# A graph layer on one Trainium2 core: 37 of 49 node blocks packed instead of 35, and sums of gathered tiles on an even beat

## The chip, the cores and the metric

The kernel runs on one core of one Trainium2 chip. The metric is the device time of one execution in microseconds; 7 executions of the kernel before have a median of 624.59 us (622.95 to 628.96). Lower is better.

## The reference, cut to what matters

6250 nodes with 128 features, 100,000 edges sorted by their target node, two kinds of edge.

```python
Xs = X[src]
m_data = Xs @ W_data.T + b_data
m_ctrl = Xs @ W_control.T + b_control
msg = jnp.where((edge_types == 0)[:, None], m_data, m_ctrl)
agg = jax.ops.segment_sum(msg, dst, num_segments=X.shape[0])
out = jax.nn.relu(agg + (X @ W_self.T + b_self))
x = _layernorm(x + out, axis=-1)
```

## The kernel before, in words

**Messages first.** Nodes are padded to 49 blocks of 128 rows. For each block the kernel multiplies x by both message weights in float32 (tile y, functions multiply, take, leave, last_part) and keeps each result as three bfloat16 parts that add up to it: the tile m3 in SBUF, and the same rows in a table in device memory, written by store. A row of 384 numbers is one node's message for one kind of edge. This build phase lasts for roughly the first 78 us.

**Then sums per target block.** Edges are sorted, so all edges of a target block lie in one window of 18 x 128 edges, of which some belong to its neighbours. There are two ways to sum a window.

- *Packed* blocks (the first 35, in 7 groups of 5). For a group, the fields of its edges are computed (edge_fields), one-hot tiles by source block are made on DVE (bucket_hots, tile hot_st), and ranks gives each edge a slot within its source block: PE adds into the accumulator acc with the constants tri and rest, DVE takes a maximum (slot, L584), 18 times in turn. fill_a and fill_b bring the edges into their slots (tile small, L621), fill_c copies them out (vs), writes them to device memory (packed), and lists the edges that found no slot, whose rows POOL fetches in one spill gather per group (mixed, L715). For each packed block the list is then read back to all partitions (rows, L739), compared to the partition number (L746), and used as weights: g_ps (gather, L775) picks the rows out of m3 with a matmul, ACT evicts them to gs (evict, L790), and add_up sums them into agg with the one-hot of the target (hot_d, L760). A block has 25 such rounds: 98 matmuls for g_ps and 100 for agg. Evictions may be given to DVE only in blocks of the last group (b >= STARTS[-1]).
- *Gathered* blocks (the last 14). For each of their 18 x 128 edges POOL fetches the message rows by an indirect DMA from the table (gather_rows, tile msg, L877, a ring of MB = 5 tiles), DVE makes a one-hot of the targets for six at a time (hot_g, L889), and gathered_sums adds the tile into agg_g with four matmuls.

All matmuls with 32 output rows go through by_columns (L231) in fours, one for each 32 columns of the weights. Every block adds its own term x @ W_self into its accumulator, and finish_blocks or finish_gathered sums its three parts (whole, L153), applies relu, adds x and takes the statistics; normalise scales and stores a group of blocks at a time.

**What sets the order.** Each part above is a Python generator that yields steps: a name, the engines that may run it with a cost, and the steps it needs. The class Order is a planner: it keeps a clock per engine (T is PE, V is DVE, A is ACT, G is POOL, S is SP), and among the steps that could start first takes the one with the earliest due time from due(). The order in which the steps are taken is the order of the instructions in each engine's queue. Nothing of the planner runs on the chip: its clocks only decide who stands ahead of whom. The constants that the change touches are BLOCK (due distance of packed blocks), PACE (due distance of gathered tiles, and before also the cost of a gather on POOL), and GROUPS, from which NPB (packed blocks), NG (gathered blocks) and the starts of the groups follow.

Of the kernel before, what the change touches and what calls it, by code (L numbers as in the profile page):

```python
# [27 lines left out]
KT = 18  # L28
# [4 lines left out]
ES = ER // RJ  # L33
EPS = 1e-05

GROUPS = (5,)*7
Q = max(GROUPS)
NPG = len(GROUPS)
NPB = sum(GROUPS)
NG = NB - NPB  # L40
STARTS = [sum(GROUPS[:i]) for i in range(NPG)]
R = 32
# [10 lines left out]
CH = 6  # L53
# [5 lines left out]
class Order:  # L59
# [10 lines left out]
    CLOSE = 0.1  # L70

    def __init__(self):
        self.free = dict.fromkeys("TVAGS", 0.0)
        self.end = {}

    def run(self, streams, due):
# [24 lines left out]
def step(name, costs, *needs, lag=0.0):  # L101
    return as_tuple(name), costs, [as_tuple(n) for n in needs], lag


def as_tuple(name):
    return name if isinstance(name, tuple) else (name,)
# [107 lines left out]
def sums_over_windows(ctx, tc, x, xt, edges, w, bias, table, packed, total,  # L214
                      add_parts, finish, load_rows, norm):
    nc = tc.nc
    V, A, G, T = nc.vector, nc.scalar, nc.gpsimd, nc.tensor
# [66 lines left out]
    for j in range(RJ):  # L284
# [17 lines left out]
    counted = {n: const.tile([P, P, n], BF16, name=f"count{n}")  # L302
               for n in sorted({DC, CH, *GROUPS})}
    tri = const.tile([P, P], BF16, name="tri")
# [77 lines left out]


    LEAD, BUILT = 6.0, 76
    BLOCK = 13.1
    PACE = 1.68
    AHEAD, FIRST = 26.0, 20

    def due(kind, *i):
# [35 lines left out]
        if kind in ("rows", "sel", "d", "g", "e", "s"):  # L425
            of = {"rows": 1, "sel": 1, "d": 2}.get(kind, NS)
            lead = {"rows": -9, "sel": -3, "d": -1, "g": 0, "e": 1, "s": 2}[kind]
            return BUILT + BLOCK * (i[0] + (i[1] / of if len(i) > 1 else 0)) + lead
        if kind in ("gh", "gm", "msg"):
            k = i[1] * CH if kind == "gh" else i[1]  # L430
            return BUILT + PACE * (i[0] * KT + k) + {"msg": 0, "gh": 2, "gm": 5}[kind]
        n = GROUPS[i[0]]
        end = BUILT + BLOCK * STARTS[i[0]] - (AHEAD if i[0] else FIRST)
        span = BLOCK * n if i[0] else 34.0
# [7 lines left out]
        if kind in ("two", "v"):  # L442
            c, k = (i[1], 0) if kind == "two" else divmod(i[1], KC)
# [71 lines left out]
    stored = [("table", g, t) for g in range(len(PARTS)) for t in range(2)]  # L515
# [337 lines left out]
    gathered = [(j, k) for j in range(NG) for k in range(KT)]  # L853
    idx = const.tile([P, NG, KT], I32, name="idx")
    rel_g = const.tile([P, NG, KT], BF16, name="rel_g")
    msgs, g_hots, kept = {}, {}, []
    GQ = -(-NG // -(-NG // Q))
    MB, XB = 5, 2

    def gathered_fields():  # L860
        yield step("idx", {"V": 1.8}, ("y", NB * 3 // 4), *[("win", b) for b in range(NPB, NB)])
# [10 lines left out]
    def gather_rows():  # L872
        for i, (j, k) in enumerate(gathered):
            free = [("gm", *gathered[i - MB])] if i >= MB else [*stored, "idx"]
            yield step(("msg", j, k), {"G": PACE}, *free, lag=3.0 - PACE)
            msgs[j, k] = late.tile([P, D3], BF16, name="msg", bufs=MB)
            G.indirect_dma_start(  # L877
                out=msgs[j, k], out_offset=None, in_=table[:, :],
                in_offset=bass.IndirectOffsetOnAxis(ap=idx[:, j, k : k + 1], axis=0),
            )  # L880

    def gathered_hots():
        chunks = [(j, c) for j in range(NG) for c in range(KT // CH)]
        for i, (j, c) in enumerate(chunks):

            free = [("gm", chunks[i - XB][0], chunks[i - XB][1] * CH + CH - 1)] if i >= XB else []
            yield step(("gh", j, c), {"V": 0.55}, ("msg", j, c * CH), ("counts", CH), *free)
            g_hots[j, c] = hot = late.tile([P, P, CH], BF16, name="hot_g", bufs=XB)
            V.tensor_tensor(hot, counted[CH],  # L889
                            rel_g[:, j, None, c * CH : c * CH + CH].to_broadcast([P, P, CH]),  # L890
                            op=ALU.is_equal)

    def gathered_sums():
        for j, k in gathered:
            free = [("agg", NPB + j)] if k == 0 else [("o", NPB + j)] if k == KT - 1 else []
            yield step(("gm", j, k), {"T": 0.165}, ("msg", j, k), ("gh", j, k // CH), *free)
            if k == 0:
                aggs[NPB + j] = ps_a.tile([P, D3], F32, name="agg_g")
            by_columns(aggs[NPB + j], g_hots[j, k // CH][:, :, k % CH], msgs.pop((j, k)),
                       start=k == 0, stop=k == KT - 1, skip_group_check=True)  # L900

    def finish_gathered():
        for j in range(NG):
            b = NPB + j
            yield step(("whole", b), {"V": 0.5}, ("gm", j, KT - 1))
            whole = add_parts(aggs.pop(b), work)
            yield step(("sum", b), {"V": 0.7}, ("whole", b))
            if j % GQ == 0:
                kept.append((late.tile([P, GQ, D], F32, name="h_g"),
                             work.tile([P, Q, 2], F32, name="mv_g")))  # L910
            h, mv = kept[-1]
            finish(h[:, j % GQ, :], whole, xss.pop(b))
            stats(mv[:, j % GQ, :], h[:, j % GQ, :], work)
# [14 lines left out]
    def close_build():  # L928
# [9 lines left out]
        normalise([(lambda g=g: (hs_[g], mvs[g]), STARTS[g] + q0, q0, n) for g, q0, n in PIECES], "p"), add_up(), gather(), evict(), to_hots(), bucket_hots(),  # L938
        multiply(), take(0, "yh", "y"), leave(0, "y1", "yh"),
        take(1, "ym", "y1"), last_part(), constants(), store(), close_build(), add_counts(),  # L940
        finish_gathered(), gathered_sums(), gathered_hots(), gather_rows(), gathered_fields(),
        normalise([(lambda i=i: kept[i], NPB + i * GQ, 0, min(GQ, NG - i * GQ))
                   for i in range(-(-NG // GQ))], "g"),
        load_own("p", list(range(NPB)), XS),
# [128 lines left out]
```

## Time and profile before

| What | Value |
|---|---|
| median of 7 executions | 624.59 us |
| the profiled execution's own time | 626.73 us |
| its span | 625.0 us |
| mean granted clock of TensorE over the span | 0.982 |

The profile is of one execution. A row of a group reads: line, engine, operation, output and inputs, shapes and count, then the busy time in us and the mean ns of one, then the idle time of that engine just before them with what ended it. PE is the matmul part of TensorE and PEld its weight loads; DVE, ACT, POOL and SP are the vector, scalar, GpSimd and sync engines. Ends of matmuls are modelled, so their starts say more than their lengths. A row of waits reads: who waited for whom, us in total, how often, the longest.

These groups of the page name the work of the gathered blocks and of the evictions:

```profile
L790 ACT CAST gs<-g_ps 128x384 bf16<-128x384 f32 x807 | 337.6, 495 | 148.3 <-PE g_ps L775 90.3
L877 POOL DMA_INDIRECT msg<-table,idx x252 | 283.7, 1126 | 201.8 <-PE g_ps L775 87.7
L231 PE MATMUL agg<-gs,hot_d 128*32 128x384 bf16 x3360 | 307.8, 337 | 18.7 <-ACT gs L790 11.3
```

### The profile page before, as it was taken

The numbers are of one execution on the slowest core, as the hardware profiler recorded it, in microseconds if no ns is written. First come the engines' busy times: TensorE is split into PE (matmuls) and PEld (weight loads), VectorE is DVE, ScalarE is ACT, GpSimd is POOL, SyncE is SP. The second block draws the span as 40 slices with busy tenths as digits, with TensorE's granted clock in tenths as the row PEclk, the third lists the DMA queues.
The fourth block names the chain that finished last, engine by engine and source line by source line (L and its number), as shares of the span: only waits on it lengthen the run. The fifth ranks groups of instructions, "written<-read, shape, count | busy, mean of one in ns | idle before, by whom it ended". The sixth has DMA issues, their size and how long they took to land.

```text
span 625.0 us, 26355 instructions
## 1 busy us (share of the span) xinstructions
PE 549.3 (88%) x11204; PEld 442.4 (71%) x11204; DVE 433.8 (69%) x967; ACT 420.2 (67%) x1003; POOL 292.5 (47%) x267
## 2 busy tenths in 40 slices
PE   6899878997989898898999899899898999878994
PEld 4455565776768776677868787778786887766883
DVE  4778794768575777767678766878677656447784
ACT  6644553667587766668767786677777777667784
POOL 1000016555556565655555664656645465465510
PEclk9899987999999999999999999999999999999998
DMA  3576764324334333344243443434334343335401
GB/s 104 151 221 182 228 234 134 108 70 155 95 110 130 113 105 116 118 134 147 66 162 114 143 123 108 120 113 142 119 118 130 114 142 118 118 108 161 141 13 43
DMA packets 60932, 79.19 MB, mean 127 GB/s; under 512 B 15760, under 2 KB 51371, under 8 KB 60807
## 3 DMA queue, kind: packets, MB, share of 16 engines
q1 hardware_dynamic: 47253, 49.14, 24.7%
q0 software_dynamic: 12400, 25.08, 14.2%
q10 hardware_dynamic: 1154, 3.21, 1.7%
q8 instruction: 89, 1.46, 0.9%
q14 instruction: 36, 0.29, 0.1%
HBM read 64.35 MB, written 13.05 MB: 124 GB/s over the span
## 4 chain that ended last, share of the span: by engine, by line
PE 77%; ACT 7%; DVE 6%; issue 5%; DMA 3%; SPq 1%; another core or an unknown queue 0%; ACTq 0%; DVEq 0%
PE agg L231 26%; PE g_ps L775 25%; PE acc L231 9%; PE agg_g L231 8%; PE small L621 6%; ACT gs L790 5%; PE y L465 2%; DVE hot_st L567 1%; DVE slot L584 1%; ACT h_p L189 1%; DMA rows<-packed 1%; DVE two L605 1%; DMA packed<-vs 1%; DMA msg<-table,idx 1%; ACT h_g L189 0%
## 5 line engine op out<-in xcount | busy, mean ns | idle before, releaser
L790 ACT CAST gs<-g_ps 128x384 bf16<-128x384 f32 x807 | 337.6, 495 | 148.3 <-PE g_ps L775 90.3
L877 POOL DMA_INDIRECT msg<-table,idx x252 | 283.7, 1126 | 201.8 <-PE g_ps L775 87.7
L775 PE MATMUL g_ps<-m,rows 128*32 128x384 bf16 x3430 | 335.5, 335 | 23.1 <-issue 11.3
L231 PE MATMUL agg<-gs,hot_d 128*32 128x384 bf16 x3360 | 307.8, 337 | 18.7 <-ACT gs L790 11.3
L231 PEld LDWEIGHTS <-hot_d 128*32 128x32 bf16 x3500 | 204.2, 137 | 59.3 <-issue 49.8
L775 PEld LDWEIGHTS <-rows 128*32 128x32 bf16 x3430 | 189.1, 138 | 53.0 <-issue 47.9
L584 DVE TENSOR_REDUCE slot<-acc 128x5 bf16<-128x490 f32 x126 | 83.7, 664 | 65.8 <-PE acc L231 31.7
L231 PE MATMUL agg_g<-msg,hot_g 128*32 128x384 bf16 x1008 | 106.6, 330 | 3.8 <-DMA msg<-table,idx 3.4
L760 DVE TENSOR_TENSOR hot_d<-count,to 128x1664 bf16<-128x1664 bf16 x70 | 74.5, 1066 | 12.7 <-PE agg L231 7.3
L621 PE MATMUL small<-hot_st,two 128*32 128x98 bf16 x1260 | 69.8, 290 | 2.2 <-issue 2.0
L231 PE MATMUL acc<-hot_st,tri 128*32 128x490 bf16 x504 | 61.4, 377 | 3.1 <-DVE hot_st L567 2.2
L621 PEld LDWEIGHTS <-two 128*32 128x32 bf16 x1260 | 56.4, 117 | 6.7 <-issue 4.9
L231 PE MATMUL acc<-hot_st,rest 128*32 128x490 bf16 x476 | 56.5, 380 | 4.4 <-DVE slot L584 3.5
L231 PEld LDWEIGHTS <-hot_g 128*32 128x32 bf16 x1008 | 52.8, 125 | 6.9 <-issue 5.7
L715 POOL DMA_INDIRECT mixed<-table,row_i x7 | 6.5, 934 | 95.7 <-PE g_ps L775 82.7
L153 DVE TENSOR_REDUCE whole<-agg 128x128 f32<-128x384 f32 x35 | 19.4, 555 | 44.8 <-PE g_ps L775 34.4
L476 ACT CAST m<-y 128x512 bf16<-128x512 f32 (+1 forms) x50 | 28.1, 577 | 31.0 <-PE y L483 23.1
L567 DVE TENSOR_TENSOR hot_st<-count,st_b 128x2940 bf16<-128x2940 bf16 x21 | 41.9, 2000 | 9.1 <-PE small L621 4.9
L746 DVE TENSOR_SCALAR rows<-rows,pid 128x3136 bf16<-128x3136 bf16 x35 | 36.1, 1033 | 2.5 <-DMA rows<-packed 2.4
L465 PE MATMUL y<-w_sb,xt 128*128 128x256 f32 x98 | 33.3, 426 | 0.0
L231 PEld LDWEIGHTS <-rest 128*32 128x32 bf16 x476 | 21.6, 100 | 12.6 <-issue 11.7
L790 DVE CAST gs<-g_ps 128x384 bf16<-128x384 f32 x33 | 17.9, 556 | 12.6 <-PE g_ps L775 10.4
(144 smaller groups left out, 437.8 us busy)
## 6 DMA issues: line engine op xcount, KB each, us to landing
rows<-packed SPq DMA_DIRECT2D x35, 784.0 KB
table<-m SPq DMA_DIRECT2D x10, 768.0 KB
msg<-table,idx POOLq DMA_INDIRECT x252
xt<-in_xt ACTq DMA_DIRECT2D x5, 512.0 KB
xt_p<-in_xt SPq DMA_DIRECT2D x35, 64.0 KB
xs_p<-in_x SPq DMA_DIRECT2D x35, 64.0 KB
out<-h_p SPq DMA_DIRECT2D x6, 320.0 KB
table<-m SPq DMA_DIRECT2D x2, 480.0 KB
```

Of the source, the lines that this page charges most:

```text
L153: nc.vector.tensor_reduce(whole, agg.rearrange("p (i c) -> p c i", i=3), axis=AX.X, op=ALU.add)
L231: T.matmul(out[c : c + 32], lhsT[:, c : c + 32], rhs, **flags)
L465: T.matmul(y[:, j, :], xts[g][:, b + j - at_part[g], :], w_sb[:, : 2 * D], start=j == 0, stop=False, skip_group_check=True)
L476: A.copy(part_of(b, n, i), ys[b][:, :n, :].rearrange("p b (t c) -> p t b c", t=2))
L567: V.tensor_tensor(hot, counted[n][:, None, 1 : NT + 1, :].to_broadcast([P, KC, NT, n]), fields[grp][2][:, c * KC : c * KC + KC, None, :].t ...
L584: V.tensor_reduce(slots[grp][:, k, :], by_q, axis=AX.X, op=ALU.max)
L621: T.matmul(vt[c0 : c0 + R, q // 2, :], two[:, k % KC, i, :, q], hot[:, k % KC, :, q], start=k == 0 and q < 2, stop=k == KT - 1, skip_group ...
L746: V.tensor_scalar(rows[b], rows[b], pid1, None, op0=ALU.is_equal)
L760: V.tensor_tensor(hot, counted[DC][:, :, :n], places[grp][:, q, None, c * DC : c * DC + n].to_broadcast([P, P, n]), op=ALU.is_equal)
L775: T.matmul(g_ps[t * R : (t + 1) * R, :D3], rows[b][:, :, s], m3[:, s, :], start=True, stop=True)
L790: (A.copy if e == "A" else V.tensor_copy)(gs[at], g_tiles.pop((b, g))[at, :D3])
L877: G.indirect_dma_start(out=msgs[j, k], out_offset=None, in_=table[:, :], in_offset=bass.IndirectOffsetOnAxis(ap=idx[:, j, k : k + 1], axis=0),
```

## The change

Two blocks more are packed (37) and two fewer gathered (12). The groups are now eight: two of four blocks, five of five, one of four. The planner gets a further clock, C, that belongs to no engine: a stream of beats takes PACE of it for each gathered tile, one after the other, and the sum of a gathered tile needs its beat. A gather costs POOL 1.25 in the planner's eyes, where it was PACE. The ring of gathered tiles has four places and not five, so a gather waits for the sum four back. BLOCK, PACE and the due time of gathered sums get other numbers.

```diff
-GROUPS = (5,)*7
+GROUPS = (4,)*2+(5,)*5+(4,)
...
-        self.free = dict.fromkeys("TVAGS", 0.0)
+        self.free = dict.fromkeys("TVAGSC", 0.0)
...
-    BLOCK = 13.1
-    PACE = 1.68
+    BLOCK = 12.7
+    PACE = 2.1
...
+        if kind in ("beat", "beating"):
+            return 0.0
...
-            return BUILT + PACE * (i[0] * KT + k) + {"msg": 0, "gh": 2, "gm": 5}[kind]
+            return BUILT + PACE * (i[0] * KT + k) + {"msg": 0, "gh": 2, "gm": 0}[kind]
...
-    MB, XB = 5, 2
+    MB, XB = 4, 2
...
-            yield step(("msg", j, k), {"G": PACE}, *free, lag=3.0 - PACE)
+            yield step(("msg", j, k), {"G": 1.25}, *free, lag=3.0)
...
+    def beats():
+
+        yield step("beating", {"C": 4.0}, *stored, "idx")
+        for i, (j, k) in enumerate(gathered):
+            yield step(("beat", j, k), {"C": PACE}, "beating")
...
-            yield step(("gm", j, k), {"T": 0.165}, ("msg", j, k), ("gh", j, k // CH), *free)
+            yield step(("gm", j, k), {"T": 0.165}, ("msg", j, k), ("beat", j, k), ("gh", j, k // CH), *free)
```

Lines of the changed kernel after the new rule in due() stand two lower than before (L775 is L777, L877 is L879).

What this does to the queues, at three places. First POOL, whose whole work after the start is gathers: msg rows for the gathered blocks, and one spill gather (mixed) per group. The lines with a minus are those of before.

```order
-L715 DMA mixed_146<-table,row_i_1182 32x384
-L877 DMA msg<-table,idx 128x384 x29
-L715 DMA mixed_147<-table,row_i_3056 32x384
-L877 DMA msg<-table,idx 128x384 x41
-L715 DMA mixed_146<-table,row_i_5325 32x384
+L717 DMA mixed_147<-table,row_i_1160 32x384
+L879 DMA msg<-table,idx 128x384 x19
+L717 DMA mixed_148<-table,row_i_2633 32x384
+L879 DMA msg<-table,idx 128x384 x25
+L717 DMA mixed_147<-table,row_i_4421 32x384
```

Between the spill gathers of the first groups there were 29 and 41 gathers, and now there are 19 and 25. In all, 252 gathers become 216, and 7 spill gathers become 8.

Second PE in the first packed block (agg), where the first gathered tile (msg) is summed into agg_g. Before:

```order
L775 MATMUL g_ps_1584<-m3_157,rows_1124 32x384
...
L231 LDWEIGHTS hot_g_1566
L231 MATMUL agg_g_1591<-msg_1434,hot_g_1566 32x384
...
L231 MATMUL agg_1339<-gs_1559,hot_d_1323 32x384
```

And now:

```order
L777 MATMUL g_ps_1670<-m3_159,rows_1081 32x384
...
L231 LDWEIGHTS hot_g_1645
L231 MATMUL agg_g_1677<-msg_1440,hot_g_1645 32x384
...
L231 MATMUL agg_1296<-gs_1620,hot_d_1307 32x384
```

The neighbours are of the same kind, but the place in the queue is later: 23 fours of g_ps, 19 of agg and 56 of acc stood ahead of this sum, and now 27, 23 and 62.

Third PE in the middle of the program. Each line stands for the first matmul of a four. Before, about a third of the way into the queue:

```order
L775 MATMUL g_ps_6083<-m3_157,rows_5198 32x384
...
L231 MATMUL agg_g_5730<-msg_5919,hot_g_6056 32x384
...
L231 MATMUL agg_g_5730<-msg_5971,hot_g_6056 32x384
...
L231 MATMUL agg_5943<-gs_6054,hot_d_5269 32x384
```

And now, at about the same place:

```order
L231 MATMUL agg_g_5478<-msg_6145,hot_g_6245 32x384
...
L777 MATMUL g_ps_6435<-m3_159,rows_5364 32x384
...
L777 MATMUL g_ps_6446<-m3_159,rows_5364 32x384
...
L777 MATMUL g_ps_6455<-m3_159,rows_5364 32x384
...
L231 MATMUL acc_6158<-hot_st_4978,tri_144 32x490
...
L231 MATMUL agg_g_5478<-msg_6209,hot_g_6245 32x384
```

Two gathered sums stood back to back there, which they did at 13 places in the program and now do at 4; between those shown now stand three rounds of the packed block, the copies of the group's slots and a rank step. A packed block in the middle had 7 to 9 gathered sums in its stretch of PE's queue, and now has 4 to 8, mostly 6. The last gathered sum stood 45 rounds of agg before the end of the queue, and now stands 25 before it.

More of the change, by code (lines that the diff above doesn't have):

```diff
@@ L940, in sums_over_windows @@
         take(1, "ym", "y1"), last_part(), constants(), store(), close_build(), add_counts(),
-        finish_gathered(), gathered_sums(), gathered_hots(), gather_rows(), gathered_fields(),
+        finish_gathered(), gathered_sums(), gathered_hots(), gather_rows(), gathered_fields(), beats(),
         normalise([(lambda i=i: kept[i], NPB + i * GQ, 0, min(GQ, NG - i * GQ))
```

## The prediction, made before the changed kernel had run

> **What bounds the kernel now.** I read the page first: which engine is busy, and through which engine the chain runs that ended last.
>
> ```profile
> span 625.0 us, 26355 instructions
> PE 549.3 (88%) x11204; PEld 442.4 (71%) x11204; DVE 433.8 (69%) x967; ACT 420.2 (67%) x1003; POOL 292.5 (47%) x267
> PE 77%; ACT 7%; DVE 6%; issue 5%; DMA 3%; SPq 1%; another core or an unknown queue 0%; ACTq 0%; DVEq 0%
> ```
>
> PE is the busiest engine and carries 77% of the chain. POOL, whose gathers are what the change spaces out, is busy for less than half. Next I cut the span into stages by the end of the packed blocks. Each block ends with the DVE sum of its accumulator (whole, L153), so the first and last start of that line, and the start for block 28, are the marks.
>
> ```profile
> L153 DVE TENSOR_REDUCE whole<-agg x35: 524/557/558, 103.2 to 616.6; 128x128 f32<-128x384 f32 x35
> 551.01 0.56 DVE L153 TENSOR_REDUCE whole<-agg 128x128 f32<-128x384 f32 x1 [1.76 <-PE g_ps L775]
> 0.00:103.20 103.20, 85.03 (x988) 54.45 (x989) 70.89 (x165) 54.01 (x105) 11.01 (x17) 0.93 0.61 180
> 103.20:551.00 447.80, 403.84 (x8869) 336.35 (x8866) 314.49 (x685) 312.72 (x768) 254.72 (x228) 1.00 0.40 121
> 551.00:616.60 65.60, 60.42 (x1350) 51.59 (x1349) 46.03 (x106) 52.82 (x129) 26.78 (x24) 1.00 0.30 94
> ```
>
> The columns after the length are the busy time of PE, PEld, DVE, ACT and POOL, then the granted clock. The middle stage holds 28 blocks in 447.8 us, so 16.0 us a block, with PE busy for 403.84, which is 14.4 of each 16.0. ACT has 11.2 and DVE 11.2. The last six blocks, with no ranks left to make, take 65.6 us, 10.9 each. PE is the engine that is nearest to full in every stage. Then the waits, to see whether gathers hold anyone up.
>
> ```profile
> POOL msg L877 <- PE g_ps L775: 87.7, 114, 2.3
> POOL msg L877 <- PE agg_g L231: 79.0, 66, 2.9
> ACT gs L790 <- PE g_ps L775: 90.3, 135, 5.4
> PE agg L231 <- ACT gs L790: 11.3, 25, 1.7
> PE g_ps L775 <- ACT gs L790: 10.9, 20, 1.1
> PE agg_g L231 <- DMA msg<-table,idx: 3.4, 1, 3.4
> DVE slot L584 <- PE acc L231: 31.7, 31, 4.3
> ```
>
> POOL waits for PE for 166.7 us in these two rows alone, ACT waits for PE for 90.3. PE waits for a gathered tile once in 252 gathers. So today the gathers follow PE and cost it only their matmuls. This is the fact on which my forecast rests: the spacing of gathers can take little from PE, while the two blocks that move from gathered to packed give it more to do.
>
> **The change, part by part.** I call four matmuls, one for each 32 rows of the output, a quartet. Its price on PE is the distance from one start to the next where PE runs without a pause. These rows give it: a 384-column quartet, a 490-column one, and 52 of the 98-column matmuls of the bucket fill.
>
> ```profile
> 603.05 0.39 PE L231 MATMUL agg<-gs,hot_d 128*32 128x384 bf16 x4
> 603.21 0.39 PE L775 MATMUL g_ps<-m,rows 128*32 128x384 bf16 x4
> 308.24 0.39 PE L231 MATMUL acc<-hot_st,tri 128*32 128x490 bf16 x4
> 308.45 0.34 PE L231 MATMUL agg_g<-msg,hot_g 128*32 128x384 bf16 x4
> 82.05 1.81 PE small L621 x52
> ```
>
> That is 0.16 us, 0.21 us and, from 1.81 us for 52, 0.035 us each. The counts of before stand in these groups; those of the change follow from its loops and its order.
>
> ```profile
> L775 PE MATMUL g_ps<-m,rows 128*32 128x384 bf16 x3430 | 335.5, 335 | 23.1 <-issue 11.3 <-ACT gs L790 10.9
> L231 PE MATMUL agg_g<-msg,hot_g 128*32 128x384 bf16 x1008 | 106.6, 330 | 3.8 <-DMA msg<-table,idx 3.4 <-issue 0.2
> L231 PE MATMUL acc<-hot_st,tri 128*32 128x490 bf16 x504 | 61.4, 377 | 3.1 <-DVE hot_st L567 2.2 <-issue 0.8
> L621 PE MATMUL small<-hot_st,two 128*32 128x98 bf16 x1260 | 69.8, 290 | 2.2 <-issue 2.0
> ```
>
> 1. *Two more packed blocks.* g_ps grows by 98 matmuls a block, agg by 100: 396 matmuls, 99 quartets, 99 x 0.16 = **+15.8 us**.
> 2. *Two gathered blocks fewer.* 1008 becomes 864 matmuls, 36 quartets less: 36 x 0.16 = **-5.8 us**. The own term of a block (x @ W_self) is paid either way.
> 3. *Ranks.* Seven groups of five blocks have 7 x 35 = 245 quartets of 490 columns (126 with tri, as the row shows in matmuls, and 119 with rest). The new groups have 175 of 490 and 105 of 392. For 392 columns I estimate 0.21 x 392/490 = 0.168. 175 x 0.21 + 105 x 0.168 - 245 x 0.21 = **+2.9 us**.
> 4. *Bucket fill.* 36 matmuls a block, 72 more: 72 x 0.035 = **+2.5 us**.
>
> Sum of PE's own work: **+15.4 us**. None of it lies beside other PE work, since PE is one queue in order. Only PE's waits could hide it. One packed block of before costs PE 49.5 x 0.16, with 7.2 gathered quartets x 0.16, 7 rank quartets x 0.21 and 36 x 0.035, and 0.5 us as an allowance for its own term, which no row here prices: 12.3 us. The middle stage takes 16.0. So some 3.6 us of each block are waits and hand-overs.
>
> 5. *Waits of the added blocks.* Between 0 (all new work falls into waits that exist) and 2 x 3.6 = 7.2 us (each block brings its waits along). I take **+5**, nearer the row of the middle stage, because the added blocks stand there. The 16.0 us of that stage is the nearest thing measured.
> 6. *Evictions by DVE in the last group.* The planner may give an eviction to DVE only in blocks of the last group, which has four blocks now, five before.
>
> ```profile
> L790 DVE CAST gs<-g_ps 128x384 bf16<-128x384 f32 x33 | 17.9, 556 | 12.6 <-PE g_ps L775 10.4 <-PE agg_g L231 0.7 <-ACT gs L790 0.6
> 568.09 3.93 ACT L790 CAST gs<-g_ps 128x384 bf16<-128x384 f32 x10 [0.72 <-PE g_ps L775]
> ```
>
> 33 / 5 = 6.6 evictions go back to ACT at about 0.38 us each (ten in 3.93 us, the last one's length taken off): 0 to 2.5 us, I take **+1**, since ACT still has pauses there.
>
> 7. *The start.* PE comes to the first gathered sum before its tile is there.
>
> ```profile
> 90.65 0.88 POOL L715 DMA_INDIRECT mixed<-table,row_i  x1 [82.73 <-PE g_ps L775]
> 91.83 1.53 POOL L877 DMA_INDIRECT msg<-table,idx  x1 [0.30 <-ACT gs L790]
> 95.06 0.53 PE L231 MATMUL agg_g<-msg,hot_g 128*32 128x384 bf16 x4 [3.43 <-DMA msg<-table,idx]
> 92.00:96.00 4.00, 0.94 (x16) 0.76 (x19) 2.68 (x13) 0.96 (x2) 3.26 (x3) 0.71 0.20 55
> 96.00:100.00 4.00, 4.00 (x56) 2.33 (x50) 0.00 (x0) 0.48 (x1) 2.91 (x4) 0.50 0.26 74
> L584 DVE TENSOR_REDUCE slot<-acc 128x5 bf16<-128x490 f32 x126 | 83.7, 664 | 65.8 <-PE acc L231 31.7 <-PE g_ps L775 25.3 <-PE agg_g L231 4.6
> ```
>
> PE stands still for 3.43 us, and right after it the granted clock is 0.71 and 0.50 for two stretches of 4 us, about 4 x 0.29 + 4 x 0.50 = 3.2 us of full speed lost. In the new order eight 384-column quartets and six rank quartets more stand ahead of that first sum, some 2.4 us of work that would fill most of the pause. Also the first group has four blocks: its 18 rank reductions go from 0.664 to about 0.53 us, up to 2.4 us earlier, which brings PE there sooner and takes some of the filling back. So between 0 and -(3.4 + 3.2) = -6.6 us; I take **-3**. The Trainium skill (TensorE: Matmul & The Clock Gate, Part 1) says that the clock falls to half after an idle window of about 3.4 us. The two rows agree; by that rule a pause cut below it would save the 3.2 whole, by a free-running window only sometimes.
>
> 8. *Waiting for the fourth sum back, and the even beat.* The beat exists in the planner alone; on the chip it is only another order. Behind a gather that waits on POOL stand only the next gathers and the spill gather of the next group, for whose tile the last sum of each block of that group waits on PE; no engine but PE waits for POOL. In the new order, priced as above, a gathered sum comes every 2.0 us of PE work on the median (1.5 before), four of them 8 us, against some 3.5 us from the moment POOL was free for the first gather (90.65 + 0.88) to PE's matmul at 95.06. So a ring of four still covers it: 0. Thirteen pairs of gathered sums stood back to back, four do now; one quartet less in the way of an eviction is 9 x 0.16 = 1.4 us at most, and I take 0.
>
> Sum: 15.4 + 5 + 1 - 3 = **+18.4 us**, on the profiled execution's span 625.0 -> 643.4, its time 626.73 -> 645.1. That execution lies 2.1 us above the median of 624.59, so I forecast 624.59 + 18.4 = **643 us**. ACT and DVE do not become the bound: two more middle blocks bring each 2 x 11.2 = 22 us, and both stay near 11.2 of 16.0, 70%.
>
> Ends of this case: low, 15.4 + 0 + 0 - 6.6 - 1.4 = +7.4, 632. High, 15.4 + 7.2 + 2.5 and one more group boundary, priced by the longest single wait of DVE for a rank quartet (4.3, in the rows of waits): +29.4, 654.
>
> **Rivals.**
>
> *A, faster.* PE's waits for ACT's evictions are 11.3 + 10.9 = 22.2 us. If clumped gathered sums cause them, because they delay the quartet that an eviction waits for, the even spacing removes them. All of it: 15.4 - 22.2 - 3 = -9.8, 615 us. It decides from 12.4 of the 22.2 on. For it: the pairs back to back go from 13 to 4, and ACT waits 90.3 us for g_ps. Against it: a clump delays by 0.16 us only, and 50 more evictions are added. I give it 0.10.
>
> *B, hidden.* PE has 44 us without a matmul in the middle stage, and busy time is modelled. If the added work falls into these pauses whole, 15.4 - 15.4 + 1 - 3 = -2, 622 to 627 us. The Trainium skill (Perfetto Trace Analysis, Identifying the Most-Contended Engine) calls matmul busy time a poor measure and reads load-weight busy time instead; by that PE has 29% left, not 12%, and this rival is the likelier for it. The quartets that start 0.16 us after one another, for a length of 0.39 each, speak against it: the queue has no gap there to fill. I give it 0.08.
>
> *C, the ring too short.* If a gather's way takes over four beats (8 us), PE waits in each round of four: 54 rounds, so every us above 8 costs 54 us, over 654 at once. The one wait of 3.4 us in 252 speaks against it. I give it 0.03.
>
> **How the numbers follow.** My case 0.79, A 0.10, B 0.08, C 0.03. A measurement of this kernel can tell about 0.5% (3 us) from no change. Over 627.7 lie my case, C and nothing else: slower 0.82; B gives within 0.5%: 0.08; A gives faster: 0.10. The range must hold 0.8: my case from 632 to 654 holds about 0.75 of its 0.79, so it reaches down to 627, over the upper part of B.
>
> **What would show it.** Right: packed blocks in the middle still some 15.5 to 16 us apart, 30 of them and not 28; PE busy up by some 20 us; POOL's waits for PE longer; the pause before the first gathered sum under 3 us. Wrong: middle blocks under 15.2 us (then A: PE's waits for gs fall by half), PE busy unchanged (B), or PE waiting for msg more than a few times (C). What would break it most is a middle block that gets cheaper by over 0.6 us from two gathered sums less than its 0.3 us of matmuls says.

## The result: 605.3 us, 3.3% faster, and the profile after

| What | Before | The change |
|---|---|---|
| median | 626.42 us (46 runs) | 605.33 us (19 runs, 602.18 to 608.17) |
| ratio, 95% interval | | 0.9668, 0.9649 to 0.9688 |
| the profiled execution's own time | 626.73 us | 607.58 us |
| its span | 625.0 us | 605.9 us |

One execution of e15 below, at 613.20 us, is over 1.5% above the fastest of its kernel and is left out of that row's ratio, not of its median.

The forecast was 643 us, so it missed in sign and by 38 us. First the page of the change: span, busy time of each engine, and the chain that ended last by engine.

```profile
span 605.9 us, 27437 instructions
PE 553.2 (91%) x11683; PEld 451.5 (75%) x11683; DVE 451.9 (75%) x1039; ACT 441.7 (73%) x1058; POOL 258.4 (43%) x232
PE 80%; ACT 7%; DVE 6%; issue 3%; DMA 2%; SPq 1%; another core or an unknown queue 0%; ACTq 0%; DVEq 0%
```

PE has 479 matmuls more than before (11683 against 11204). The forecast counted 464 of them, worth 15.4 us by its prices. But PE is busy for only 3.9 us more, and the span is 19.1 us shorter. Next the stages, cut at the same marks as before: the first DVE sum of a packed block, the start for block 30 (two middle blocks more than before), and the last one. After the length come the busy times of PE, PEld, DVE, ACT and POOL, and the granted clock.

```profile
L153 DVE TENSOR_REDUCE whole<-agg x37: 545/557/558, 102.5 to 596.7; 128x128 f32<-128x384 f32 x37
529.60 0.56 DVE L153 TENSOR_REDUCE whole<-agg 128x128 f32<-128x384 f32 x1 [1.51 <-PE agg L231]
0.00:102.51 102.51, 83.11 (x1002) 51.51 (x1003) 69.55 (x173) 54.77 (x104) 8.28 (x14) 0.93 0.59 178
102.51:529.60 427.09, 406.19 (x9246) 346.64 (x9242) 332.35 (x729) 331.23 (x817) 223.68 (x193) 1.00 0.39 121
529.60:596.70 67.10, 63.93 (x1443) 53.37 (x1438) 47.62 (x128) 53.74 (x134) 26.40 (x25) 1.00 0.34 101
```

All of the gain lies in the middle: 30 blocks in 427.09 us, **14.24 us a block where it was 16.0**, with PE idle for 20.9 us of that stage where it was 44.0. The start is 0.7 us shorter, the last six blocks 1.5 us longer, the end behind them 0.8 us longer. Then the waits of PE and three groups, to hold against those of before.

```profile
PE agg L231 <- ACT gs L792: 8.4, 17, 1.6
PE g_ps L777 <- ACT gs L792: 7.3, 10, 3.0
PE agg L231 <- issue: 2.4, 6, 0.7
PE g_ps L777 <- issue: 1.6, 6, 0.5
L792 ACT CAST gs<-g_ps 128x384 bf16<-128x384 f32 x859 | 357.9, 494 | 114.9 <-PE g_ps L777 82.9
L879 POOL DMA_INDIRECT msg<-table,idx x216 | 246.7, 1142 | 236.9 <-PE agg_g L231 134.6
L231 PE MATMUL agg_g<-msg,hot_g 128*32 128x384 bf16 x864 | 90.6, 329 | 0.1
```

Of before, one row of waits goes with these that has not been shown:

```profile
PE agg L231 <- issue: 8.4, 20, 1.0
```

PE's waits for evictions fell from 22.2 to 15.7 us. Those put down to "issue", for which the profile shows no cause, fell from 19.7 (11.3 + 8.4) to 4.0. ACT evicts 52 tiles more and still idles 33 us less ahead of them (148.3 to 114.9). The pause before the first gathered sum is gone (0.1 us). So the work that was added is there, and waits all over the middle stage went. The question is which ones, and why.

### The profile page after: what moved, and what is told of

Same layout as the page of the kernel before. It is cut to its first block, busy times and chain, and to the rows that moved or that the text cites. A ratio compares the mean times of both kernels' runs of the same rounds, so it can differ in the third digit from the quotient of the medians.

```text
span 605.9 us, 27437 instructions
## 1 busy us (share of the span) xinstructions
PE 553.2 (91%) x11683; PEld 451.5 (75%) x11683; DVE 451.9 (75%) x1039; ACT 441.7 (73%) x1058; POOL 258.4 (43%) x232
## 3 DMA queue, kind: packets, MB, share of 16 engines
q8 instruction: 93, 1.52, 1.0%
## 4 chain that ended last, share of the span: by engine, by line
PE 80%; ACT 7%; DVE 6%; issue 3%; DMA 2%; SPq 1%; another core or an unknown queue 0%; ACTq 0%; DVEq 0%
PE agg L231 29%; PE g_ps L777 28%; PE acc L231 9%; PE small L623 6%; PE agg_g L231 6%; ACT gs L792 4%; DMA rows<-packed 2%; DVE slot L586 1%; DVE hot_st L569 1%; PE y L467 1%; ACT h_p L189 1%; ACT m L478 1%; ACT count L316 1%; PE y L485 1%
## 5 line engine op out<-in xcount | busy, mean ns | idle before, releaser
L792 ACT CAST gs<-g_ps 128x384 bf16<-128x384 f32 x859 | 357.9, 494 | 114.9 <-PE g_ps L777 82.9
L777 PE MATMUL g_ps<-m,rows 128*32 128x384 bf16 x3626 | 345.6, 335 | 9.4 <-ACT gs L792 7.3
L879 POOL DMA_INDIRECT msg<-table,idx x216 | 246.7, 1142 | 236.9 <-PE agg_g L231 134.6
L231 PE MATMUL agg<-gs,hot_d 128*32 128x384 bf16 x3552 | 320.7, 339 | 12.1 <-ACT gs L792 8.4
L777 PEld LDWEIGHTS <-rows 128*32 128x32 bf16 x3626 | 196.0, 138 | 39.0 <-issue 32.2
L586 DVE TENSOR_REDUCE slot<-acc 128x5 bf16<-128x490 f32 (+1 forms) x144 | 90.1, 626 | 48.1 <-PE acc L231 26.9
L231 PE MATMUL agg_g<-msg,hot_g 128*32 128x384 bf16 x864 | 90.6, 329 | 0.1
L231 PE MATMUL acc<-hot_st,rest 128*32 128x490 bf16 (+1 forms) x544 | 59.0, 366 | 9.5 <-DVE slot L586 7.8
L231 PE MATMUL acc<-hot_st,tri 128*32 128x490 bf16 (+1 forms) x576 | 64.0, 360 | 2.1 <-DVE hot_st L569 1.3
L569 DVE TENSOR_TENSOR hot_st<-count,st_b 128x2940 bf16<-128x2940 bf16 (+1 forms) x24 | 45.0, 1877 | 9.4 <-PE g_ps L777 5.0
L478 ACT CAST m<-y 128x512 bf16<-128x512 f32 (+1 forms) x50 | 28.2, 579 | 23.5 <-PE y L485 15.2
L231 PEld LDWEIGHTS <-tri 128*32 128x32 bf16 x576 | 23.8, 100 | 5.0 <-issue 4.2
```

What stands on the lines that cost most here:

```text
L231: T.matmul(out[c : c + 32], lhsT[:, c : c + 32], rhs, **flags)
L478: A.copy(part_of(b, n, i), ys[b][:, :n, :].rearrange("p b (t c) -> p t b c", t=2))
L569: V.tensor_tensor(hot, counted[n][:, None, 1 : NT + 1, :].to_broadcast([P, KC, NT, n]), fields[grp][2][:, c * KC : c * KC + KC, None, :].t ...
L586: V.tensor_reduce(slots[grp][:, k, :], by_q, axis=AX.X, op=ALU.max)
L777: T.matmul(g_ps[t * R : (t + 1) * R, :D3], rows[b][:, :, s], m3[:, s, :], start=True, stop=True)
L792: (A.copy if e == "A" else V.tensor_copy)(gs[at], g_tiles.pop((b, g))[at, :D3])
```

## What a trace shows around one gather

Here is a piece of the timeline of the kernel before. Columns: start, length, engine, line, work, and in brackets the idle time ahead and what ended it.

```profile
440.32 0.94 POOL L877 DMA_INDIRECT msg<-table,idx  x1 [0.30 <-PE acc L231]
...
440.95 0.39 PE L775 MATMUL g_ps<-m,rows 128*32 128x384 bf16 x4 [0.30 <-ACT gs L790]
...
441.85 2.01 ACT L790 CAST gs<-g_ps 128x384 bf16<-128x384 f32 x5 [0.96 <-PE g_ps L775]
441.92 0.67 DVE L584 TENSOR_REDUCE slot<-acc 128x5 bf16<-128x490 f32 x1 [0.94 <-PE g_ps L775]
442.21 0.94 POOL L877 DMA_INDIRECT msg<-table,idx  x1 [0.95 <-PE g_ps L775]
442.38 0.39 PE L775 MATMUL g_ps<-m,rows 128*32 128x384 bf16 x4 [1.04 <-issue]
```

A gather starts at 440.32. PE's quartet at 440.95 ends by its model at 441.34, but whoever waits for PE goes on only at 441.85, 1.53 us after the gather's start, ACT, DVE and POOL within 0.4 us of each other. PE starts its next quartet at 442.38, just after the first of ACT's five evictions can have ended; the profile puts this wait of 1.04 us down to "issue".

To see whether this is the rule I counted the records of PE's semaphore updates, which no view prints, around each gather that is not followed by another within 1.75 us and lasts under 1.06 us, between 103 and 530 us.

| Around a gather's start | Before | The change |
|---|---|---|
| gathers counted | 86 | 101 |
| PE's updates per us, 0.3 to 1.2 us after it | 0.47 | 0.56 |
| modelled ends of the same instructions, same stretch | 2.33 | 2.61 |
| PE's updates per us, 1.3 to 1.75 us after it | 7.0 | 6.9 |
| ACT and DVE starts released by PE, 0.5 to 1.2 us after it | 10 | 13 |
| the same, 1.3 to 1.8 us after it | 94 | 101 |

So PE finishes work evenly by its modelled ends, but its signals nearly stop for 0.9 us after a gather has begun, and then come in a burst. The Trainium skill (Perfetto Trace Analysis, Tensor Engine Instruction) says that a matmul's end in a profile is computed from its size and not observed; the trace agrees, since 2.33 ends stand against 0.47 updates, and it is why a view of PE alone does not show the hold.

The hold may not be of PE's signals alone. In the kernel before, the recorded updates of DVE and ACT in the same stretch are 0.71 and 0.66 per us, against 1.52 ends each. But many of these records are missing from the trace: 653 stand for the 827 instructions of DVE that update, and 724 for the 960 of ACT. With one gather left (e10 below) there are 826 and 959. So with the gathers the records of all three engines suffer (of PE's 1434 there are 1379), and what share of the price belongs to whose signals is not shown.

The theory, G below, later H: **each gather on POOL holds up PE's signals for about 1 us, and whoever needs one then waits.** The rivals: the work of PE in its new order (P), the transfers (T), or one of the change's parts for another reason.

## The experiments

Ratios are to the kernel before in the same set of runs, with 95% intervals. Packed and gathered blocks are 35 and 14 unless the row says otherwise.

| Run | Median us | Ratio |
|---|---|---|
| e1 every second gather left out | 587.75 | 0.9367 (0.9311 to 0.9422) |
| e2 new groups alone, 37/12 | 628.65 | 1.0049 (1.0017 to 1.0081) |
| e3 groups and slower pace, 37/12 | 630.94 | 1.0077 (1.0048 to 1.0105) |
| e4 the new order, old groups | 603.26 | 0.9640 (0.9592 to 0.9688) |
| e5 change without beat, 37/12 | 620.67 | 0.9924 (0.9890 to 0.9959) |
| e6 change, sums due later, 37/12 | 609.26 | 0.9696 (0.9648 to 0.9745) |
| e7 change, old cost, 37/12 | 608.34 | 0.9712 (0.9681 to 0.9744) |
| e8 change, ring of five, 37/12 | 609.71 | 0.9736 (0.9704 to 0.9768) |
| e9 before with beat, pace 1.8 | 620.04 | 0.9912 (0.9884 to 0.9941) |
| e10 before, one gather left | 539.16 | 0.8626 (0.8585 to 0.8668) |
| e11 e4, one gather left | 542.93 | 0.8697 (0.8664 to 0.8729) |
| e12 before, plain transfers by SP | 552.93 | 0.8838 (0.8801 to 0.8875) |
| e13 before with beat, pace 1.68 | 616.71 | 0.9823 (0.9770 to 0.9875) |
| e14 before, 64 rows a gather | 630.48 | 1.0063 (1.0031 to 1.0094) |
| e15 e4 with pace 1.75 | 608.51 | 0.9660 (0.9586 to 0.9734) |
| e16 e4 with 33/16, pace 1.52 | 629.49 | 1.0067 (1.0025 to 1.0108) |
| e17 before, memsets for gathers | 564.38 | 1.0389 (1.0343 to 1.0434) |
| e18 change with 39/10, pace 2.5 | 566.39 | 1.0421 (1.0374 to 1.0467) |

In the sets of e1 to e16 the kernel before took 625.7 to 626.6 us. In that of e17 and e18, on another occasion, it took **544.35 us**; these two stand apart, and their part below says what that means.

### Groups or order: e2, e3, e4

```diff
 e2, e3:
-GROUPS = (5,)*7
+GROUPS = (4,)*2+(5,)*5+(4,)
 e3 also:
-    PACE = 1.68
+    PACE = 2.1
```

> The kernel before with the new groups alone (37 packed blocks, 12 gathered), planner constants, ring of five and due times as before. The gathered blocks run as densely as before and are done earlier. G: 36 gathers less at about 1 us against 15.4 us of work: 603 to 615 us. E: the order is not even, so the added work shows: 635 to 643 us. S: the groups are all there is, 605 us.

> The same with PACE 2.1, which is the planner's cost of a gather on POOL and sets due times, but without the beat, with the ring of five and the old due times. G: as the run with the groups alone, some us less because gathers stand further apart: 600 to 612 us. E: the spacing is nearly that of the change, so 605 to 612 us. S: 605 us.

e4 is the change with the old groups:

```diff
-GROUPS = (4,)*2+(5,)*5+(4,)
+GROUPS = (5,)*7
-    BLOCK = 12.7
-    PACE = 2.1
+    BLOCK = 13.1
+    PACE = 1.8
```

> The change with the old seven groups of five (35 packed blocks, 14 gathered, 252 gathers): beat, ring of four, cost and due times as in the change, PACE 1.8 so that 252 beats take as long as 216 did, BLOCK 13.1. G: as many gathers as before, so 615 to 625 us. E: all of the gain without the added work, 590 to 600 us. S: 625 us.

Three theories stood at the start: G (each gather has a price), E (the even order makes the gain) and S (the new groups make it). The groups bring nothing (628.65), alone or with the slower pace (630.94), and the new order brings 22.8 us with no block moved. S falls. G expected too much of 36 gathers fewer in e2, and has no word for e4. E is near in e2 and e4, and wrong in e3: a slower pace in the planner without the beat is not an even order, or not one that helps.

### Does a gather cost time: e1, e10, e11, e12, e14

```diff
 e1:
+            if k % 2:
+                msgs[j, k] = msgs_kept[j, k - 1]
+                continue
 e10, e11:
+            if i:
+                msgs[j, k] = msgs_kept[0]
+                continue
 e12:
-            G.indirect_dma_start(
...
+            r = 29 * i % 80 * P
+            nc.sync.dma_start(msgs[j, k], table[r : r + P, :])
```

> The kernel before, with every second gather left out (the sum of an odd tile reads the tile ahead of it, so half of the gathered rows are not fetched and the gathered blocks' sums are others). PE, ACT and DVE keep every instruction and their order; POOL has 126 gathers and not 252. Theory G: in the trace of before hardly any of PE's semaphore updates is recorded from 0.3 to 1.2 us after a gather starts on POOL, and many at 1.3 us, so each gather delays what waits for PE. Then the time falls with the number of gathers: the change saved 20 us and 15.4 us of added PE work with 36 gathers less, 1.0 us a gather; at 0.5 to 1.0 us for 126 gathers, 500 to 565 us. Theory E (the even spacing of the sums on PE is what helped): 625 us, since the order of PE is unchanged. Theory S (smaller groups): 625 us.

> The kernel before with one gather of a message tile left in and the other 251 left out (all sums read the same tile); PE, ACT and DVE keep their order. Theory H (a gather on POOL holds up PE's signals to the engines that wait, and the order of the change helps by spacing these): 540 to 565, and within 1% of the next run, which has the order of the change. Theory P (the order of PE's own work makes the gain, with or without gathers): 3 to 4% above the next run.

> The order of the change with the old 7 groups (603 us with its gathers), with one gather left in and the other 251 left out. Theory H: 540 to 565, within 1% of the run ahead. Theory P: 3 to 4% below the run ahead.

> The kernel before with each of the 252 gathers of message tiles replaced by a plain transfer of 128 rows of the same table in a row, issued by SP, with the same waits; which rows a tile gets is wrong, the bytes are the same. Theory H (the time that POOL spends on the lists of a gather is what holds the signals): 540 to 575. Rival T (the transfers on the DMA engines cost the time, by competing with the others): 610 to 630. A plain transfer stands in SP's queue behind the row loads, so PE may wait for some tiles; then it is read from the waits.

126 gathers fewer saved 38 us, 0.30 us each: G's direction, under the 0.5 to 1.0 that it expected, and against E and S, for which gathers cost nothing. 251 fewer saved 86.6 us, **0.34 us each**; in the new order 60.3 us, **0.24 each** (603.26 - 542.93). Without gathers the two orders are within 0.8% of each other, and the new one is the slower. The ends hide a little of it: the last packed sum comes 3.7 us earlier in e11 than in e10 (526.1 against 529.8), and 15.0 against 8.3 us follow it. With the gathers in, it comes 32.2 us earlier in e4 than before (584.4 against 616.6). So P falls for all but some 4 us, and the gain of the order is a lower price of its gathers. Page and two groups of e10:

```profile
span 538.1 us, 25860 instructions
PE 503.7 (94%) x11204; PEld 444.7 (83%) x11204; DVE 429.4 (80%) x967; ACT 416.3 (77%) x1003; POOL 11.6 (2%) x16
L790 ACT CAST gs<-g_ps 128x384 bf16<-128x384 f32 x807 | 334.1, 498 | 71.8 <-PE g_ps L775 58.8 <-issue 3.6 <-PE agg L231 3.3
L775 PE MATMUL g_ps<-m,rows 128*32 128x384 bf16 x3430 | 325.7, 332 | 2.9 <-ACT gs L790 2.6
```

The same 11204 matmuls now keep PE busy for 503.7 us, not 549.3: 45.6 us of what the page called busy was no work. PEld stays the same (442.4, now 444.7). PE's waits put to "issue" before a g_ps, 11.3 us, are gone, and ACT's idle time before evictions has halved.

With plain transfers of the same bytes the time is 552.93, though PE now does wait for some tiles:

```profile
PE agg_g L231 <- DMA msg<-table: 13.5, 11, 2.4
```

So of the 86.6 us at most 14 are the transfers', and rival T falls; the rest goes with indirect gathers issued on POOL. The form and the issuing engine were changed together here, and no plain transfer was issued by POOL, so which of the two it is stays open.

For e14 the ring was five fixed tiles, zeroed once, and a gather took the first 64 indices.

```diff
-                out=msgs[j, k], out_offset=None, in_=table[:, :],
-                in_offset=bass.IndirectOffsetOnAxis(ap=idx[:, j, k : k + 1], axis=0),
+                out=msgs[j, k][: P // 2], out_offset=None, in_=table[:, :],
+                in_offset=bass.IndirectOffsetOnAxis(ap=idx[: P // 2, j, k : k + 1], axis=0),
```

> The kernel before, each of the 252 gathers of message tiles fetching 64 rows and not 128 (the lower half of each tile stays zero and adds nothing, which leaves these edges out); as many gathers, waits and matmuls as before. If the price of 0.34 us goes with the rows: 580 to 590. If with the number of gathers: 615 to 626. POOL's own time for one gather (0.94 us for 128 rows) should fall in the same measure.

```profile
L881 POOL DMA_INDIRECT msg<-table,idx x252 | 270.1, 1072 | 218.8 <-PE g_ps L775 91.7
```

Half the rows save nothing (630.48), and a gather takes POOL 1072 ns on the mean where it took 1126. The price goes with the number of gathers and not with their rows.

### Which part of the order: e5 to e9, e13

```diff
 e5:
-            yield step(("gm", j, k), {"T": 0.165}, ("msg", j, k), ("beat", j, k), ("gh", j, k // CH), *free)
+            yield step(("gm", j, k), {"T": 0.165}, ("msg", j, k), ("gh", j, k // CH), *free)
 e6:
-            return BUILT + PACE * (i[0] * KT + k) + {"msg": 0, "gh": 2, "gm": 0}[kind]
+            return BUILT + PACE * (i[0] * KT + k) + {"msg": 0, "gh": 2, "gm": 5}[kind]
 e7:
-            yield step(("msg", j, k), {"G": 1.25}, *free, lag=3.0)
+            yield step(("msg", j, k), {"G": PACE}, *free, lag=3.0 - PACE)
 e8:
-    MB, XB = 4, 2
+    MB, XB = 5, 2
```

> The change, but the sum of a gathered tile no longer needs its beat; ring of four, due times and costs stay, all work the same. Theory E (the even beat of the sums on PE keeps the gathers from following one another closely, and each gather holds up the signals of PE to the engines for about 1 us): 618 to 630, as before, with middle blocks of 15 us and more and the number of gathers that start under 1.6 us after the one ahead back from 18 to over 35. Theory R (the ring of four alone ties each gather to a sum): 603 to 610. Theory D (the sums come earlier in the blocks by their due time): 603 to 610.

> The change, but with the due time of a gathered sum 5 us later, as before; beat, ring and costs stay. Theory D: 618 to 628. Theories E and R: 603 to 610.

> The change, but a gather costs the planner PACE again, with the shorter lag that goes with it. The planner then lets gathers start no closer than PACE of its own clock. If the planner's view of a gather's cost makes the gain: 618 to 628. Theories E, R and D: 603 to 610.

> The change, but with a ring of five gathered tiles, so a gather waits for the sum five back and not four. Theory R (a gather tied closely to a sum, so that it never runs ahead of PE): 612 to 625, with POOL's gathers closer together. Theories E and D: 603 to 610.

Taking the beat away loses 15.3 us of 21.1, as E expected; the due time, the cost and the ring lose 3.0 to 4.4 each, within the 603 to 610 that E gave them and little above what can be told. R and D fall as causes of the whole. Then the beat alone, put into the kernel before with beats() and its clock C as the change has them; PACE is 1.8 in e9 and stays 1.68 in e13:

```diff
-            yield step(("gm", j, k), {"T": 0.165}, ("msg", j, k), ("gh", j, k // CH), *free)
+            yield step(("gm", j, k), {"T": 0.165}, ("msg", j, k), ("beat", j, k), ("gh", j, k // CH), *free)
```

> The kernel before with the beats alone: a stream of beats of 1.8, which the sums of gathered tiles need, and PACE 1.8 with it; 35 packed blocks, ring of five, due times and costs as before. Theory E (the beat makes the gain): 603 to 612. Theory E' (the beat gains only together with the shorter ring and the earlier due time): 615 to 626.

> The kernel before with the beats alone and PACE as before (1.68), so that the sums of gathered tiles end no later than before. Theory E (the beat alone gains in the middle stage, and the run with PACE 1.8 lost it at the end): 605 to 615, with an end of under 12 us behind the last packed block. Theory E' (the beat gains only with the shorter ring, the earlier due time and the new cost): 617 to 626.

The beat alone brings 9.7 us at the old pace, which is between what E and E' expected. At pace 1.8 it brings 5.7; that run stands 19.7 us behind its last packed sum, where before stood 8.4, so it gave time back at its end:

```profile
L153 DVE TENSOR_REDUCE whole<-agg x35: 546/557/559, 101.7 to 598.7; 128x128 f32<-128x384 f32 x35
span 618.4 us, 26370 instructions
```

The order's parts without the beat bring 8 us (e2 to e5), the beat on top of them 15.3.

How the beat makes a gather cheaper is only partly shown. Counted between starts on POOL from 103 us on, gathers that follow another within 1.6 us: before 44, the change 18, e4 25, e8 20, e7 26, e6 27, e15 33, e9 34, e5 36, e2 46, e13 46, e16 43. The fast kernels have few. But e3 has 32 and is the slowest of its set, and e13 has 46 and is 9.7 us faster than before: so closeness on POOL is not the whole of it. What else the beat changes, where in PE's queue a gather's hold falls, I could not take apart.

### The balance at these prices: e15, e16

```diff
 e15, against e4:
-    PACE = 1.8
+    PACE = 1.75
 e16, against e4:
-GROUPS = (5,)*7
+GROUPS = (5,)*6+(3,)
-    BLOCK = 13.1
-    PACE = 1.8
+    BLOCK = 13.9
+    PACE = 1.52
```

> The order of the change with the old 7 groups (603 us), with PACE 1.75 in place of 1.8, so that the gathered blocks end with the packed ones and not 8 us after them. By the prices found: 595 to 603; if the closer gathers cost what the end gains: 601 to 606.

> The order of the change with 33 packed and 16 gathered blocks (six groups of five, one of three), PACE 1.52, BLOCK 13.9. Two packed blocks fewer are 15.4 us less work for PE, and 36 gathers more cost 36 x 0.24 = 8.6 at the price of the even order, 36 x 0.34 = 12.4 at that of before: 590 to 600 if the even order holds its price at the closer pace; 605 or more if POOL, with 288 gathers in some 470 us, becomes too dense and the price goes back up.

Neither is better than e4, and e15 lies above both of its expected ranges. With some 15 us of PE's work less, e16 is 26 us slower than e4, and not at its end (14.5 us behind the last packed sum, 16.8 in e4). At these prices its gathers cost (629.49 - (542.93 - 15.4)) / 288 = 0.35 us each, where those of e4 cost 0.24; this is an estimate, since this balance was not run without gathers. e4 and the change cannot be told apart (0.9592 to 0.9688 against 0.9649 to 0.9688), so no version was found that is clearly faster than the change.

### A set in which gathers held nothing: e17, e18

```diff
 e17:
-            msgs[j, k] = late.tile([P, D3], BF16, name="msg", bufs=MB)
-            G.indirect_dma_start(
...
+            wide = late.tile([P, 1024], BF16, name="msg", bufs=MB)
+            G.memset(wide, 0.0)
+            msgs[j, k] = wide[:, :D3]
 e18, against the change:
-GROUPS = (4,)*2+(5,)*5+(4,)
+GROUPS = (4,)*2+(5,)*5+(3,)*2
-    BLOCK = 12.7
-    PACE = 2.1
+    BLOCK = 12.2
+    PACE = 2.5
```

> The kernel before with a memset of a tile of 128 x 1024 on POOL in place of each of the 252 gathers of message tiles, with the same waits; the gathered edges add nothing, so their messages are left out. If only the gather's own work in software holds the others: 539 to 552, as without gathers. If any work on POOL of this kind does: 590 to 625. How long one memset takes is read from the profile.

> The change with 39 packed and 10 gathered blocks (two groups of four, five of five, two of three), PACE 2.5, BLOCK 12.2. Two packed blocks more are 15 us of PE's work; 36 gathers fewer at 0.24 us each give back 8.6, and their wider distance perhaps some more: 605 to 615. If the price of a gather falls further with the distance (to 0.15): 595 to 605.

In this set the kernel before ran in 544.35 us with all of its 252 gathers, 5 us from e10, which has one. The expectations are therefore void as comparisons with 626. No trace of the kernel before was taken in this set, but that of e18 shows what is different. Two groups of its page, then ACT's wait for g_ps between 103 and 530 us in e18 and, below it, in the change, then a piece of e18's timeline:

```profile
L792 ACT CAST gs<-g_ps 128x384 bf16<-128x384 f32 x913 | 375.0, 502 | 57.0 <-PE g_ps L777 43.8
L879 POOL DMA_INDIRECT msg<-table,idx x180 | 211.7, 1176 | 216.3 <-PE g_ps L777 131.3
```

```profile
ACT gs L792 <- PE g_ps L777: 40.1, 84, 2.1
```

```profile
ACT gs L792 <- PE g_ps L777: 58.4, 92, 3.2
```

```profile
214.90 0.94 POOL L879 DMA_INDIRECT msg<-table,idx  x1 [1.85 <-PE g_ps L777]
...
215.37 0.43 PE L231 MATMUL acc<-hot_st,tri 128*32 128x490 bf16 x4
...
215.85 0.67 DVE L586 TENSOR_REDUCE slot<-acc 128x5 bf16<-128x490 f32 x1 [1.59 <-PE acc L231]
```

A gather takes POOL as long as ever and an eviction is no shorter (502 ns, 494 in the change). But DVE starts 0.05 us after the quartet's modelled end (215.80), 0.95 us after the gather's start, in the stretch in which signals nearly stood still in the other sets. Over 87 such gathers PE's updates come at 2.48 per us from 0.3 to 1.2 us after the start and at 3.01 from 1.3 to 1.75 (0.47 and 7.0 before), and ACT and DVE are released 25 times from 0.5 to 1.2 us and 19 times from 1.3 to 1.8 (10 and 94 before). In the set in which e18 shows no hold the kernel before is 82 us faster, about what leaving the gathers out saved where the hold was present: that the hold is the price of the gathers has its best support here. It belongs to the occasion and not to the kernel. Nor does the chip alone set it, if the record's chip number always names the same chip: chip 5 ran this set and, 24 minutes earlier, that of e5 to e8, in which the kernel before took 626.63 us and PE's updates came at 0.65 per us from 0.3 to 1.2 us after the gathers of e5. What sets it I can't say. In this set e18, with four blocks more packed, is 22 us slower than the kernel before. The change itself was not run there, so its place on such an occasion is open; the +3.8 us of its order without gathers (e10, e11) and the 15.4 us of its added work speak for slower than before.

e17 tells of something else: a memset takes POOL 991 ns, and the DVE comparison of rows gets longer on the mean. Whether memsets hold signals where gathers do is not shown, since this set has no hold. Here are the rows of e17 (the third gives the shortest, median and longest of the comparison in ns), then the comparison in e18 and in the kernel before:

```profile
L877 POOL MEMSET msg<- 128x1024 bf16 x252 | 245.6, 991 | 176.4 <-PE agg_g L231 155.6
L746 DVE TENSOR_SCALAR rows<-rows,pid 128x3136 bf16<-128x3136 bf16 x35 | 56.4, 1613 | 3.1 <-DMA rows<-packed 3.1
L746 DVE TENSOR_SCALAR rows<-rows,pid x35: 1005/1037/5525, 76.5 to 527.8; 128x3136 bf16<-128x3136 bf16 x35
```

```profile
L748 DVE TENSOR_SCALAR rows<-rows,pid 128x3136 bf16<-128x3136 bf16 x39 | 40.8, 1047 | 5.6 <-DMA rows<-packed 5.6
```

```profile
L746 DVE TENSOR_SCALAR rows<-rows,pid 128x3136 bf16<-128x3136 bf16 x35 | 36.1, 1033 | 2.5 <-DMA rows<-packed 2.4
```

The Trainium skill (SBUF — State Buffer, SBUF: two separate sides) says that GpSimd and DVE, in certain modes of DVE, lock a shared pair of ports against each other for a whole instruction. The trace agrees: the median is unchanged (1037 ns), but 16 of the 35 comparisons take over 1.2 us, all of them beside memsets, and the longest, 5525 ns, spans five memsets in a row. In the kernel before, 31 of the 35 lie beside a gather and none takes over 1121 ns, so this lock shows no part in what gathers cost here.

## Why the prediction was wrong, point by point

- **Steps 1 and 3 to 6, the packed blocks' work.** Right in amount as far as it can be seen: with gathers priced at 0.34 us, the new groups alone come to +15.4 - 36 x 0.34 = +3.2, and e2 measured +2.6 (628.65 - 626.04). The +5 of waits a block brings along (5) and the +1 of evictions (6) are not needed for that sum. They were not tried alone.
- **Step 2, two gathered blocks fewer, was mis-sized**: -5.8, their matmuls alone. Each gather held the others for 0.34 us on top, so -5.8 - 12.2. It rested on the sentence "today the gathers follow PE and cost it only their matmuls", read from PE waiting for a tile once in 252. That view asks whether gathers come late. They never did; they held up signals between other engines.
- **Step 8, the even beat and the ring, "0", is the step that failed.** The order is worth -22.8 (e4), and without gathers +3.8 (e10, e11). The sum of the two parts tried singly, +2.6 - 22.8 = -20.2, is close to the -21.1 measured. "No engine but PE waits for POOL" was true, and no argument: nobody needs to wait for POOL to be held by it. The ring was right as far as it went, since PE did not wait for tiles.
- **Step 7, the start.** The 3.43 us pause before the first gathered sum went, as said (eight and six quartets are 2.5 us at the forecast's prices, not 2.4). Its worth of -3 did not come through: the first packed sum is 0.7 us earlier. PE stood idle for 3.43 us of 88 to 96 us before and still does for 3.24, now in several waits of the packed block, and the clock still falls. These are two of the stretches of 4 us in the change, with columns as above:

```profile
92.00:96.00 4.00, 2.35 (x31) 1.60 (x31) 2.54 (x5) 2.22 (x6) 0.37 (x1) 0.58 0.13 39
96.00:100.00 4.00, 4.00 (x94) 3.21 (x88) 3.86 (x14) 2.29 (x6) 0.00 (x0) 0.57 0.00 0
```

- **Rival A had the sign and the place** (middle blocks under 15.2 us; 14.24), with a mechanism that was too small: it had a clump delay by one quartet of 0.16 us, where the traces show a gather hold signals for about 1 us. That clumps are what the beat removed is only partly shown. PE's waits for evictions did not halve (22.2 to 15.7); the waits put to "issue" fell by more.
- **Rival B's reading was nearer than I gave it.** I dismissed it because quartets start 0.16 us apart where PE runs without a pause. That holds there, but 45.6 us of PE's busy time went with the gathers while load-weight time stayed. What the page said (busy time of matmuls is a poor measure) was borne out. **Rival C** did not occur.

The mistake common to 2 and 8: 3.6 us of each middle block (3.7 by the forecast's own terms) were booked as "waits and hand-overs" and carried along as a constant, and 19.7 us of PE's waits stood under "issue", a name for no cause. That was the place to ask what ends them.

## What to carry to other kernels

Price an instruction on a side engine by leaving it out, not by who waits for it: here 251 gathers cost 86.6 us of 626, and PE had waited for a gathered tile once. When several engines stop together and go on together, with idle time put to "issue", look for what began about a microsecond earlier, on whichever engine. And measure on more than one occasion: the same kernel took 626 us in four sets of runs and 544 in the fifth.

## What was not expected of the hardware

An indirect gather on POOL nearly silences PE's signals from 0.3 to 1.2 us after its start (0.47 updates per us against 2.33 modelled ends), then they come at 7 per us; its price of 0.34 us is per gather, not per row (64 rows: no gain, 1072 against 1126 ns). Plain transfers of the same bytes by SP have no such price (552.93 us). In one set of runs the trace of e18 shows no hold, and the kernel before took 544.35 us. PE's busy time can hold time that is not work: 45.6 us of it, 8%, went with the gathers.
